# Three edits to the order of work in a two-layer graph and mixture-of-experts kernel: the last pair's shares, the last full block of layer 0, the stores of finished tiles

## The chip, the cores and the metric

The kernel runs on one core of one Trainium2 chip. The metric is the device time of one execution in microseconds (us). Before the change the median of three runs is 1194.18 us, and they lie between 1194.14 and 1195.82. The engines are named as the profile names them: PE (TensorE, matrix products; PEld is its loading of weights), DVE (VectorE), ACT (ScalarE), POOL (GpSimd) and SP (SyncE, which here only starts transfers). A "q" behind a name (SPq, ACTq) is the engine's sequencer, which starts DMA transfers.

## The reference: what is computed

There are N = 3327 nodes with 256 features, padded to 26 tiles of 128. Two layers are computed, each a graph aggregation and then a mixture of eight experts of which each node uses two. In short:

```python
# layer 0
x = x + relu(adj @ (layernorm(x) @ W) + b)
xn = layernorm(x);  top2, idx = top_k(xn @ Wg.T + bg, 2);  p = softmax(top2)
x = x + sum_k p[k] * (relu(xn @ W1[idx_k].T + b1[idx_k]) @ W2[idx_k].T + b2[idx_k])   # hidden 1024
# layer 1
f = tanh(adj * adj) * (adj > 0), only the 700 largest entries of each row kept
x = x + relu(f @ (tanh(layernorm(x) @ Wp + bp) @ Wg1) + bg1)
xn = layernorm(x);  w = softmax(xn @ R.T);  best two, renormalised
x = x + xn + sum_k w[k] * (gelu(xn @ w1[idx_k] + b1[idx_k]) @ w2[idx_k] + b2[idx_k])   # hidden 256
```

All of it is float32.

## The kernel before

**Aggregation.** The adjacency matrix streams through six buffers `ring0` to `ring5` in pieces of 13 x 256 columns. Layer 0 (`aggregate_first`, L482) works on 13 panels of 256 nodes, the inner ones in pairs by Strassen-Winograd with seven half products. The last panel, number 12, is alone: `rest` (L558) goes through its 26 steps of `add` and, at step `first + behind_`, calls `finish`, which weighs the sums of the pair before it (panels 10 and 11) by the weight matrix (`weigh`, L503: products `ps_o`, then `add_relu` on DVE), lists the pair before that one (`listed`), and routes panels 10 and 11 (`route0`: layer norm, scores, ranks). `behind_` is `LAST_BEHIND`, 8 before. Layer 1 (`aggregate`, L430) has the plain form.

**Routing.** A pair of panels is routed on DVE (scores L662, ranks L691 to L717, the difference of the two best scores L727) and listed afterwards by `list_tokens` (L759): ACT takes the exponential of that difference (L762), DVE makes the two shares of it (`shares`, L733 to L738), PE counts the places of each node (`pr`, L770 and L771), DVE turns these into row numbers, and POOL scatters the rows into a list per expert in DRAM.

**Experts.** Blocks of 256 nodes of one expert (128 for the small "single" ones) are run by `step` (L1341) of `experts`, in the order of a plan that is made on the chip. A block is: transposes of its rows (`ptb`, L1172, copied by ACT at L1176), the hidden products `ps_h` (L1224, eight of them in layer 0) each followed by ReLU or GELU on ACT (L1232), and the output products `ps_y`. These have two forms. `second` (L1301) makes two sums of eight products each (L1321) and then adds the bias and weighs by the share on DVE (L1328, L1329). `second_seven` (L1256) takes seven half-size products (L1272); it needs sums of the weights from DVE, made by `prepare` (L1182: t1, t2, t4, t3 at L1191 to L1194, held in the buffer `gate`), sums of the hidden values (`difference` L1215, and L1263 to L1265), and eight additions L1279. Both forms end in `put`: POOL scatters the rows of the output to DRAM (`ys`, L793). Layer 0 has 30 blocks in its usual course, 0 to 29; 12, 17, 22 and 27 are single ones. From block 3 on, all full blocks of layer 0 take the seven products (`seven=3`).

**Around the first block.** Block 0 runs right after panel 12. Its `step` is given `between=finish_last`: the weighing of panel 12, the listing of panels 10 and 11 and the routing of panel 12, traced between the hidden products of block 0 and the transposes of block 1. The transposes `ptb`, `ps_h` and `ps_o` share two PSUM buffers (pool `psh`), so each waits for an earlier one to be read.

**From layer 0 to layer 1.** In the usual arm of a branch (L1723 to L1735) blocks 26 and 27 run, `add_begun` adds the expert outputs of the first 12 tiles to x on DVE (L1410, six additions), block 28 runs, `statistics` makes the layer-norm statistics of these tiles, and block 29 runs. `between` (L1626) then normalises all tiles (L371), transposes them (`pt` L387), and makes the features of layer 1 (`ps_p` L1614, `ps_s` L395). From tile 12 on it first reads the expert outputs back from DRAM (`ring<-ys`, started by SP at L1396), which has to follow all scatters, and adds them (L1410).

**End of layer 1.** In the usual arm (L1752 to L1788) blocks 8 to 31 run. From the count `at` = 18 on (the number of blocks started) SP reads outputs of finished pairs of tiles back, one pair a block; DVE adds the pair two blocks later (`add_loaded`), and ACT starts the store of the finished rows to the output (L1759).

**Order.** The code is traced in program order; then the Tile framework puts each engine's instructions in an order by a schedule of its own, in which something that is ready sooner can be issued before something written earlier. `tc.issue_after(i)`, and `behind(list)` with the last instruction of the list, keep what is traced inside behind instruction i, but only what runs on i's own engine. `last_product` holds PE's last product, `last_hidden` ACT's last ReLU or GELU, `last_y` DVE's last operation on an output. Semaphores follow from the data.

## Time and profile before

| what | us |
|---|---|
| median of three runs (lowest, highest) | 1194.18 (1194.14, 1195.82) |
| the profiled execution, its time | 1194.71 |
| its span, first to last instruction | 1192.9 |
| PE busy in the span | 1152.2 (97%) |
| DVE busy | 871.1 (73%) |
| ACT busy | 557.6 (47%) |
| POOL busy | 295.4 (25%) |

By stages, from the times of the span:

| stage, us | length | PE busy |
|---|---|---|
| 272.0 to 300.0: panel 12 | 28.0 | 27.09 |
| 300.0 to 313.6: block 0 up to its output products | 13.6 | 11.03 |
| 313.6 to 640.0: blocks 0 to 25 | 326.4 | 326.17 |
| 640.0 to 684.5: blocks 26 to 28 | 44.5 | 43.88 |
| 684.5 to 698.8: block 29 | 14.3 | 11.80 |
| 698.8 to 753.0: features of layer 1 | 54.2 | 52.77 |
| 753.0 to 1047.0: aggregation of layer 1 | 294.0 | 294.00 |
| 1047.0 to 1128.0: blocks of layer 1 | 81.0 | 79.94 |
| 1128.0 to 1163.0: blocks of layer 1 beside the read-back | 35.0 | 28.30 |
| 1163.0 to 1193.0: single blocks and the last outputs | 30.0 | 11.41 |

How to read it: a line of the timeline has the start, the duration, the engine, the line of the code, the operation, what it writes and reads, and how often; behind it in brackets the time that the engine stood idle just before, and what ended that. A line of the waits has the total, the number and the longest. One float32 product is two MATMUL records. Idle time of an engine matters only where the work that ends the stage stands behind it.

### The profile page before, as it was taken

Reading aid. Unit: us, or ns where it says so; the run is one execution under the profiler, and the core shown is the slowest. Engines: PE = TensorE matmul, PEld = TensorE weight load, DVE = VectorE, ACT = ScalarE, POOL = GpSimd, SP = SyncE. Lnnn points to the kernel's source line nnn. Section 1 sums busy time; section 2 is a strip of 40 time slices with the busy share of each in tenths; the row PEclk is TensorE's granted clock in tenths of the full one; section 3 lists DMA queues with packets and bytes.
Section 4 is the critical chain, followed back from the end, with each engine's and each line's share of the span. In section 5 each row is a group of like instructions: output and inputs, shape, how many; then the busy total and the mean of one; then the engine's idle time right before and its main releaser. Section 6 shows DMA issues by size and latency. Waiting matters only on the chain. (4 is left out here: it accounts for less than half of the span.)

```text
span 1192.9 us, 19772 instructions
## 1 busy us (share of the span) xinstructions
PE 1152.2 (97%) x6241; PEld 1005.0 (84%) x6241; DVE 871.1 (73%) x3013; ACT 557.6 (47%) x1053; POOL 295.4 (25%) x367
## 2 busy tenths in 40 slices
PE   8999999999999999999999999999999999999973
PEld 7888888888788888888888877888888888888863
DVE  7698999988875555554545669389999998785454
ACT  5689657440223333334333345985564552043321
POOL 2111332243331111111111111022233223265432
PEclk9999999999999999999999999999999999999996
DMA  9995738734376556757575936154454451478686
GB/s 350 178 278 248 250 126 234 252 104 147 122 256 226 187 190 194 259 182 266 191 232 172 370 142 259 63 186 160 167 195 156 180 185 59 130 243 258 209 282 218
DMA packets 123185, 241.68 MB, mean 203 GB/s; under 512 B 24480, under 2 KB 93120, under 8 KB 116160
## 3 DMA queue, kind: packets, MB, share of 16 engines
q1 hardware_dynamic: 108656, 205.59, 52.8%
q0 software_dynamic: 11136, 31.60, 7.1%
q10 hardware_dynamic: 3280, 3.15, 0.8%
q8 instruction: 51, 0.84, 0.3%
q14 instruction: 62, 0.51, 0.1%
HBM read 203.98 MB, written 36.33 MB: 201 GB/s over the span
## 5 line engine op out<-in xcount | busy, mean ns | idle before, releaser
L440 PE MATMUL ps_g<-s,ring 128*128 128x256 f32 x1352 | 294.2, 380 | 0.0
L440 PEld LDWEIGHTS ps_g<-s,ring 128*128 128x128 f32 x1352 | 256.0, 190 | 34.4
L1232 ACT ACTIVATE pad<-ps_h,ring 128x256 f32<-128x256 f32 (+1 forms) x282 | 128.9, 458 | 286.9 <-PE ps_h L1224 147.4
L1224 PE MATMUL ps_h<-pad,ring 128*128 128x256 f32 (+1 forms) x1184 | 254.7, 368 | 4.5 <-ACT pad L1176 4.2
L1224 PEld LDWEIGHTS ps_h<-pad,ring 128*128 128x128 f32 x1184 | 201.1, 191 | 47.3 <-ACT pad L1232 11.5
L793 POOL DMA_INDIRECT ys<-pad,index x114 | 117.0, 1027 | 366.5 <-DVE pad L1279 250.4
L662 DVE SCALAR_TENSOR_TENSOR rt_product<-xn,gate 128x256 f32<-128x256 f32 x400 | 195.4, 488 | 16.1 <-ACT xn L360 2.8
L793 POOL DMA_INDIRECT xlist<-xn,rt_idx x104 | 115.3, 1109 | 153.4 <-DVE ln_nw L347 58.0
L1486 ACT ACTIVATE sign<-ring,below 128x416 bf16<-128x416 f32 x208 | 133.4, 641 | 11.9 <-DMA ring<-in_adjT 6.0
L470 PE MATMUL ps_g<-ring,pad 128*128 128x256 f32 x520 | 115.1, 380 | 2.0 <-DMA ring<-in_adjT 2.0
L470 PEld LDWEIGHTS ps_g<-ring,pad 128*128 128x128 f32 x520 | 98.4, 190 | 15.6 <-DMA ring<-in_adjT 2.4
L1651 ACT ACTIVATE ring<-ring 128x3328 f32<-128x3328 f32 x22 | 65.4, 2977 | 87.4 <-DVE ring L1650 56.3
L1279 DVE SCALAR_TENSOR_TENSOR pad<-ps_y,ring,pad 128x128 f32<-128x128 f32 x184 | 61.9, 348 | 47.9 <-PE ps_y L1272 47.7
L470 PE MATMUL ps_g<-ring,s 128*128 128x256 f32 x390 | 89.6, 379 | 0.0
L470 PEld LDWEIGHTS ps_g<-ring,s 128*128 128x128 f32 x390 | 74.1, 190 | 10.1
L480 DVE TENSOR_TENSOR ring<-ring,ring 128x768 f32<-128x768 f32 (+1 forms) x80 | 79.6, 1013 | 0.0
L495 PE MATMUL ps_g<-ring,s 128*128 128x256 f32 x312 | 68.5, 380 | 3.1 <-ACT s L360 3.1
L495 PEld LDWEIGHTS ps_g<-ring,s 128*128 128x128 f32 x312 | 59.0, 190 | 11.6 <-ACT s L360 3.7
L1652 ACT ACTIVATE ring<-ring 128x3328 f32<-128x3328 f32 x22 | 65.4, 2977 | 0.6
L1263 DVE TENSOR_TENSOR xnT<-pad 128x512 f32<-128x512 f32 x23 | 15.9, 691 | 59.5 <-ACT pad L1232 59.5
L776 POOL COPY xn<-rt_w 128x4 f32<-128x4 f32 x26 | 4.9, 199 | 211.1 <-DVE rt_w L738 211.1
L1321 PE MATMUL ps_y<-s,pad 128*128 128x256 f32 (+1 forms) x200 | 49.6, 388 | 0.1
(240 smaller groups left out, 1595.6 us busy)
## 6 DMA issues: line engine op xcount, KB each, us to landing
ring<-in_adjT SPq DMA_DIRECT2D x50, 1664.0 KB, 8.9
ring<-in_f_w1T SPq DMA_DIRECT2D x30, 1024.0 KB, 5.6
ring<-in_f_w2T SPq DMA_DIRECT2D x30, 1024.0 KB, 9.1
ring<-xlist SPq DMA_DIRECT2D x52, 258.0 KB, 3.5
ring<-in_f_w SPq DMA_DIRECT2D x36, 256.0 KB, 3.6
ring<-ys SPq DMA_DIRECT2D x12, 512.0 KB, 4.7
ring<-in_f_b SPq DMA_DIRECT2D x34, 128.0 KB, 8.2
xlist<-h2T SPq DMA_DIRECT2D x16, 257.0 KB, 13.8
```

The lines of the kernel that those rows point to most:

```text
L440: nc.tensor.matmul(ps[it], lhsT=chunks[k][:, c, ts(it, P)], rhs=s[:, j, :], start=(j == 0), stop=(j == NT - 1),)
L470: nc.tensor.matmul(ps, lhsT=b[:, c, :], rhs=a[:, c, :], start=(first and c == 0), stop=(c == CJ - 1), skip_group_check=not first,)
L480: nc.vector.tensor_tensor(out[:, part, :], out[:, part, :], other[:, part, :], ALU.add)
L495: nc.tensor.matmul(sums[pan][c], lhsT=s[:, j, ts(c, P)], rhs=piece(pan, j // CJ)[:, j % CJ, :], start=(j == 0), stop=(j == NT - 1),)
L662: nc.vector.scalar_tensor_tensor(product, xn, 1.0, gate[:, e, :], ALU.mult, ALU.mult, accum_out=sc[:, g, e : e + 1],)
L793: d = nc.gpsimd.indirect_dma_start(out=a[:, :], out_offset=bass.IndirectOffsetOnAxis(ap=index, axis=0), in_=rows_, in_offset=None,)
L1224: last_product[:] = [nc.tensor.matmul(ps, lhsT=w1[:, c, ts(hc, P)], rhs=xT[:, c, :], start=(c == 0), stop=(c == DC - 1),)]
L1232: nc.scalar.activation(hT[:, hc, :], ps, func, bias=bb1[:, hc : hc + 1])
L1279: last_y[:] = [nc.vector.scalar_tensor_tensor(part, ps, xb[:, g, WT : WT + 1], part, ALU.mult, ALU.add)]
L1486: nc.scalar.activation(sign, piece(pan, k)[:, :, ts(i, GROUP)], AF.Sign, bias=below, accum_out=positive[:, pan, i, k : k + 1],)
L1651: nc.scalar.activation(a, a, AF.Square)
L1652: nc.scalar.activation(a, a, AF.Tanh)
```

## The change

It has three parts.

1. `LAST_BEHIND` goes from 8 to 11: the call of `finish` in panel 12 comes three steps later. And what is traced in `between` of block 0 is no longer kept behind PE's last hidden product, but behind ACT's last ReLU of the block, so the edge now holds for ACT's instructions and no longer for PE's.
2. The range of blocks by seven products ends before the last full block: block 29 of layer 0 takes `second`, with eight products a sum, instead of `second_seven`. The weight sums of block 28 (`prepare`) are traced ahead of `add_begun` instead of inside `step`.
3. The store of a finished pair of tiles in layer 1 is traced two blocks after its addition, not one.

```diff
-BEHIND, LAST_BEHIND = 5, 8
+BEHIND, LAST_BEHIND = 5, 11
...
         def prepare(t):
 
+            if not seven or t not in seven or groups_of(t) < SG:
+                return None
             w2 = loaded[t][4]
...
+        ahead = {}
+
+        def prepare_next():
+
+            t = len(started)
+            ahead[t] = prepare(t)
+
         def step(late, end=always, place=None, between=None):
...
-            sums = prepare(t) if seven and t >= seven and groups_of(t) == SG else None
+            sums = ahead.pop(t) if t in ahead else prepare(t)
             hT = first(ready.pop(t), w1, bb1, groups_of(t), sums)
             if sums:
                 y = weighed_bias(t)
             if between:
-                with behind(last_product):
+                with behind(last_hidden):
                     between()
...
-        nc.scalar.copy, BLOCKS0, seven=3,
+        nc.scalar.copy, BLOCKS0, seven=range(3, EARLY + LATE_PAIRS + FIXED[0] - 1),
...
         layer0.step(late)
         layer0.step(late)
+        layer0.prepare_next()
         with behind(last_y):
             add_begun()
         layer0.step(late)
...
+            def store_added(until):
+                while added and added[0][1] <= until:
+                    t, n = added.pop(0)[0]
+                    nc.scalar.dma_start(out=rows_of(out, t, n), in_=x[:, t : t + n, :])
+
             while len(layer1.started) < layer1.always:
                 layer1.step(late1)
                 at = len(layer1.started)
-                for tiles in added:
-                    nc.scalar.dma_start(out=rows_of(out, *tiles), in_=x[:, tiles[0] : sum(tiles), :])
-                added.clear()
+                store_added(at - 2)
...
                         add_loaded(yt, *tiles)
-                        added.append(tiles)
+                        added.append((tiles, at))
...
-            assert not (waiting or added)
+            assert not waiting
+            store_added(at)
```

More of the change, by code (lines that the diff above doesn't have):

```diff
@@ L1391, in experts @@
             state=state, back_to=back_to, know=know, know_rest=know_rest,
-            turn_first=turn_first, tiers_done=tiers_done(), always=always,
+            turn_first=turn_first, prepare_next=prepare_next, tiers_done=tiers_done(), always=always,
         )
```

## The prediction

> **What bounds the kernel now.** I read the page first: PE is busy for 97% of the span, so what counts is where PE stands, and what follows the last product. Then PE's waits over the whole span, of which these two lie in the stages that the edits touch.

> ```profile
> PE ps_o L506 <- ACT pad L1232: 2.6, 1, 2.6
> PE ps_y L1272 <- DVE gate L1193: 2.5, 1, 2.5
> ```

> The timeline at the first:

> ```profile
> 306.34 0.47 ACT L1232 ACTIVATE pad<-ps_h,ring 128x256 f32<-128x256 f32 x1 [0.39 <-PE ps_h L1224]
> 309.98 0.20 ACT L762 ACTIVATE rt_d<-rt_d 128x4 f32<-128x4 f32 x1 [3.17 <-DVE rt_d L727]
> 310.09 0.46 ACT L1232 ACTIVATE pad<-ps_h,ring 128x256 f32<-128x256 f32 x1
> ...
> 310.60 2.07 PE L506 MATMUL ps_o<-proj_sb,xnT 128*128 128x256 f32 x4 [2.57 <-ACT pad L1232]
> 312.47 0.21 PE L770 MATMUL pr<-rt_both,before 128*128 128x8 bf16 x1
> ```

> ACT stands 3.17 us before the exponential, which waits for DVE; the last ReLU of block 0, whose products ended at 307.17, is behind it, and PE waits for its PSUM buffer. The stage table by microseconds shows what else that costs: PE's clock is halved.

> ```profile
> 311.00:312.00 1.00, 1.00 (x3) 0.77 (x3) 0.63 (x2) 0.00 (x0) 0.25 (x2) 0.50 0.00 0
> ```

> (The 0.50 is the granted clock.) The second wait, in PE's timeline of block 29:

> ```profile
> 689.78 1.05 PE L1272 MATMUL ps_y<-ring,pad 128*128 128x128 f32 x8
> 693.33 1.16 PE L1272 MATMUL ps_y<-gate,pad 128*128 128x128 f32 x8 [2.50 <-DVE gate L1193]
> ```

> and the chain that ended last, after it:

> ```profile
> 707.17 5.63 DMA ring<-ys
> 712.90 1.24 DVE x L1410
> ```

> DVE makes the statistics of 12 tiles (12 x 0.39 us) before block 29's weight sums, and PE stands. The read-back starts only at 707.17, after the last scatter of block 29 (POOL, 701.35), and from 712.90 DVE's chain sets the pace: it asks for tile 12's transpose at 720.22, PE was free at 719.45. Last, the tail:

> ```profile
> 1136.57 0.69 DVE L1410 TENSOR_TENSOR x<-x,ring 128x512 f32<-128x512 f32 x1
> ...
> 1137.30 0.39 ACTq L1759 DMA_DIRECT2D out_x<-x  x1
> ...
> 1137.78 0.59 ACT L1176 COPY pad<-ptb 128x512 f32<-128x512 f32 x1 [2.63 <-DVE pad L1328]
> ...
> 1138.42 1.99 PE L1224 MATMUL ps_h<-pad,ring 128*128 128x256 f32 x8 [1.66 <-ACT pad L1176]
> ```

> The store waits for the addition, the copy stands behind the store, PE behind the copy.

> [...] 2.57 us idle, then half clock from about 310.2 to 313.7. [...] Here the last scatter took 5.82 us from its start to the read-back's (701.35 to 707.17); I use that.

> **Part 1, block 0.** `LAST_BEHIND`: PE's products `ps_o` waited 0.92 us (at 283.15) for DVE's L403; three steps later (12 records x 0.22 = 2.6 us) DVE has caught up, so 0.92 us goes. But panels 10 and 11 reach DVE later. PE came to `finish` at 280.06 and now at 282.7; the last of four L403, at 285.52, needs the fourth `ps_o`, which ends about 282.7 + 0.2 + 16 x 0.25 = 286.9, so near 287.2 with its own wait for L404, and fewer statistics are interleaved. I take +1.45 us for the rest of that DVE chain (bounds 1.0 and 2.6), which has no slack: scores and ranks run from 290.69 to 309.95 almost without a gap. The edge: ACT's last ReLU no longer stands behind the exponential. Block 0's products end at 307.17 - 0.92 = 306.25, the second pair of `ps_o` ends near 307.9. Then PE wants the listing products `pr`, which need DVE's counts: 310.0 + 1.45 = 311.45, in place of 312.47. Gain 1.0 us, if what lies between `pr` and the output products (1.15 us at half clock) stays as it is; the half clock may well come again, for PE idles some 3 us. The wait is so replaced by one for DVE. With the edge gone on PE, though, the framework may let block 0's output products pass `pr`. Then nearly all of the stage's loss could go: without a stall they would start at 307.9 + 0.24 + 0.44 = 308.6 against 313.62. Bounds: a loss of 0.6 us (the transposes of block 1 wait for L403, which stands behind the shares, at 312.6) and a gain of 4. I take 1.0. PE has no other wait until 640, so this shift arrives whole; queued behind ACT's exponential is then only the copy L1176. The moved `finish` also issues eight scatters on POOL (from 283.56, 1.28 us apart); they start some 0.7 us later, and what POOL makes next is not needed before the scatters at 315.48.

> **Part 2, block 29.** Removed from DVE: four weight sums and `difference` (5 x 0.68), three hidden sums (3 x 0.69), eight L1279 (8 x 0.35), in all 8.3 us; added two L1328 and L1329, 2 x (0.42 + 0.35) = 1.5 us. From ACT two L1209 (0.9 us). On PE 56 records at 0.111 (eight every 0.89 us: 694.33, 695.22) are 6.23 us; eight products are 32 at 0.216 (320.55 to 327.46 for 32 records) = 6.91, so 0.68 us dearer. The 2.50 us wait goes. So does 0.56 us at 677.35, where PE waited for ACT's copy because block 28's t4 came only at 678.5: `prepare` of 28 now goes ahead of the six additions (6 x 1.22), done near 673, while the hidden sums, behind the same DVE work as before, come at the same time (covered by block 29's hidden products as fillers; without them about 1 us). From 689.78 to 698.79 PE took 9.01 us; now 6.91. So PE is free for the transposes at 698.79 - 2.10 - 0.56 = 696.1. DVE's statistics end near 692, before that.

> What the end of the stage hangs on is the last scatter: it was held to 701.35 by the last L1279 and by the `gate` load that POOL issued between both scatters (700.46), since block 29 was reading `gate`. Now `gate` is free after block 28, and the scatter follows the last product by 0.20 + 0.46 + 0.63 us (as at 334.81 to 336.10): 697.4. That is 3.9 us earlier; read-back at 703.3, landed 708.9, tile 12 ready at 716.3; PE, 20.66 us of work after 696.1, at 716.8. Then PE's pace of 7.8 us for four tiles meets DVE's 8.05 (720.22, 728.27, 736.32), and after three groups DVE's chain, 3.9 us earlier, decides. The filters of layer 1 are queued behind these same instructions and move along, and the aggregation is all PE (294.00 of 294.00). Gain 3.9 us; bounds 2.0 (if DVE puts block 29's outputs ahead of the normalised tiles, PE waits 1.9 us) and 4.3.

> **Part 3, the stores.** Seven stores of 256 KB, 0.38 us of ACT's queue each, in the same number. All seven stand in the trace where their addition ends; five are issued even before the copy L1176 that is traced ahead of them. So the framework issues a store when it is ready, and tracing it later need not move it. Likeliest value 0. If it does move: ACT no longer stands, PE gains its waits of 3.6 us for L1176 and the 3.1 us before 1163.17. But DVE stays on its loop of scatter, 5.2 us, read-back, 4.2 to 5.9 us, addition. I estimate 2.8 us; bounds -0.5 and 3.5. The last store is traced four blocks before the end, so none delays the final outputs.

> **Sum.** 1.0 + 3.9 + 0 = 4.9 us: the profiled execution from 1194.71 to 1189.8 (span 1188.0), the median, 0.53 us lower, to 1189.3.

> **Rivals.**
> (a) As above: 1189.3, within 1188.0 to 1190.8. Chance 0.40.
> (b) The stores do move: 2.8 us more, 1186.5. For: PE's waits for ACT; against: the order seen in the trace. 0.17.
> (c) Block 0 gives nothing, as `pr` and the half clock take it all (-0.6 to 0.5): 1190.3. For: DVE's gapless chain. 0.15.
> (d) The transition gives half, with DVE's order as the new wait: 1191.7, on the border. Against: normalising is ready 3 us before PE. 0.11.
> (e) The order barely changes, or the gain is lost to transfers: 1193.5. 0.06.
> (f) Slower: without the edge on PE, the `pr` products are issued ahead of block 0's hidden products. PE would stand until 311.5, then do 6.91 + 1.8 + 0.4 us: outputs at 320.6 against 313.62, 7.0 us lost, up to 8.7 with the half clock; 1198. It decides (over 6.3 us lost) if fewer than three of eight hidden units stand ahead of them. For: ACT's order shows that the schedule took DVE's ranks to be ready too early; against: by one unit, not five. 0.11.

> **How the numbers follow.** 0.2%, 2.4 us, is about what a measurement tells from no change: 1191.8 and 1196.6. Faster: 0.40 + 0.17 + 0.15 - 0.02 + 0.04 of (d) = 0.74; same: the rest of (c) and (d), and (e) = 0.15; slower 0.11. The range leaves out (f), the top of (e) and the lowest part of (b): 1185.3 to 1193.4.

> **What would show it.** Part 1: the exponential after the ReLU in ACT's order, no wait at 283, `ps_o` without a wait, and one before `pr`. Part 2: 32 records L1321 in block 29 with no wait; POOL's `gate` load ahead of its scatters; read-back some 4 us earlier against the start of block 29; no PE wait for L371. Part 3: stores still just after their addition. Wrong: `pr` inside the hidden products, DVE's L371 behind L1328, or a shift at 753 that the tail gives back.

## The result, and the profile after

The changed kernel takes 1190.43 us (median of 6 runs, 1188.28 to 1192.74); the kernel before, run beside it, takes 1195.32 us (6 runs, 1194.14 to 1196.85). The ratio is 0.9959, with a 95% interval of 0.9944 to 0.9973: 4.9 us faster. The prediction was 1189.3 us within 1185.3 to 1193.4. The profiled execution of the changed kernel is the slowest of its six: 1192.74 us, with a span of 1191.0 against 1192.9 before, so the pair of profiles shows only 1.9 us. I come back to where the other 3 us are.

PE's waits over the whole span of the changed kernel, the longest in total first (total, number of times, longest):

```profile
PE ps_g L495 <- ACT s L360: 4.4, 2, 2.4
PE ptb L1172 <- ACT pad L1234: 4.2, 3, 3.1
PE ps_h L1226 <- ACT pad L1176: 4.1, 3, 2.6
PE pr L770 <- DVE rt_both L700: 3.1, 1, 3.1
...
PE ps_y L1274 <- DVE xnT L1265: 0.8, 1, 0.8
```

Both waits that the prediction quoted are gone: `ps_o` for ACT's ReLU (2.6) and `ps_y` for `gate` (2.5). Two new ones stand there: `pr` for DVE (3.1), in block 0, and `ps_y` for a hidden sum (0.8), in block 28. (Lines behind the edits are numbered 2 to 10 higher than before: L1232 is now L1234, L1272 L1274, L1321 L1323, L1396 L1405, L1759 L1769.)

Block 0, from PE's and ACT's timelines of the changed kernel (start, duration, engine and line; in brackets the idle time before and what ended it):

```profile
306.71 1.89 PE L506 MATMUL ps_o<-proj_sb,xnT 128*128 128x256 f32 x8
306.91 0.47 ACT L1234 ACTIVATE pad<-ps_h,ring 128x256 f32<-128x256 f32 x1 [0.39 <-PE ps_h L1226]
...
311.67 0.17 PE L770 MATMUL pr<-rt_both,before 128*128 128x8 bf16 x1 [3.07 <-DVE rt_both L700]
...
311.75 1.09 PE L1172 MATMUL ptb<-ident,ring 128*128 128x128 f32 x4
312.64 2.60 PE L1323 MATMUL ps_y<-ring,pad 128*128 128x256 f32 x6
...
313.37 0.21 ACT L762 ACTIVATE rt_d<-rt_d 128x4 f32<-128x4 f32 x1
```

The last ReLU now stands ahead of the exponential L762, and all eight `ps_o` records run without a wait. PE then stands 3.07 us for DVE's counts. The table by microseconds shows the clock after it (the 0.50 is the granted clock, the bracketed counts are instructions):

```profile
312.00:313.00 1.00, 1.00 (x5) 0.98 (x5) 1.00 (x6) 0.12 (x1) 0.14 (x1) 0.50 0.00 0
```

The output products' first six records take 2.60 us, where six at full clock took 1.46 in a second profile of this kernel.

Blocks 28 and 29, and what follows, from the timelines of PE, POOL, SP and DVE of the changed kernel:

```profile
680.86 2.09 PE L1274 MATMUL ps_y<-gate,xnT 128*128 128x128 f32 x16 [0.82 <-DVE xnT L1265]
...
686.81 0.58 POOL L320 DMA_DIRECT2D gate<-gate  x1
...
690.24 7.07 PE L1323 MATMUL ps_y<-ring,pad 128*128 128x256 f32 x32
...
697.15 1.04 PE L387 MATMUL pt<-ident,xn 128*128 128x128 f32 x8
...
698.74 0.97 POOL L793 DMA_INDIRECT ys<-pad,index  x1 [1.67 <-DVE pad L1331]
...
701.42 0.93 SPq L1405 DMA_DIRECT2D ring<-ys  x2
...
707.02 2.49 DVE L1419 TENSOR_TENSOR x<-x,ring 128x1024 f32<-128x1024 f32 x2 [3.66 <-DMA ring<-ys]
```

Block 29 is 32 records in a row; the `gate` load goes out 13.65 us earlier (686.81 for 700.46), the read-back 5.75 us earlier (701.42 for 707.17). From 697.15 to the aggregation at 748.68 PE never waits for DVE again.

The tail, from the timeline of the changed kernel:

```profile
1134.65 0.38 ACTq L1769 DMA_DIRECT2D out_x<-x  x1
1135.13 0.59 ACT L1176 COPY pad<-ptb 128x512 f32<-128x512 f32 x1 [3.55 <-DVE pad L1330]
...
1135.77 1.99 PE L1226 MATMUL ps_h<-pad,ring 128*128 128x256 f32 x8 [2.57 <-ACT pad L1176]
```

It is the picture of before: store, copy, PE behind both. ACT's whole order after 1043 us is, row for row, that of before; and with the line of part 3 set back by one block, every engine's instruction order is compiled the same. Part 3 changed nothing on the chip.

### The profile page after: what moved, and what is told of

Read it like the earlier page. It is cut to its first block, busy times and chain, and to the rows that moved or that the text cites. A ratio compares the mean times of both kernels' runs of the same rounds, so it can differ in the third digit from the quotient of the medians.

```text
span 1191.0 us, 19704 instructions
## 1 busy us (share of the span) xinstructions
PE 1152.0 (97%) x6217; PEld 1005.4 (84%) x6217; DVE 867.1 (73%) x3001; ACT 557.0 (47%) x1051; POOL 290.5 (24%) x367
## 5 line engine op out<-in xcount | busy, mean ns | idle before, releaser
L1234 ACT ACTIVATE pad<-ps_h,ring 128x256 f32<-128x256 f32 (+1 forms) x282 | 128.9, 458 | 287.2 <-PE ps_h L1226 156.1
L1281 DVE SCALAR_TENSOR_TENSOR pad<-ps_y,ring,pad 128x128 f32<-128x128 f32 x176 | 59.3, 348 | 47.5 <-PE ps_y L1274 47.3
L495 PE MATMUL ps_g<-ring,s 128*128 128x256 f32 x312 | 70.2, 386 | 4.4 <-ACT s L360 4.4
L495 PEld LDWEIGHTS ps_g<-ring,s 128*128 128x128 f32 x312 | 60.1, 194 | 13.5 <-ACT s L360 5.2
L1323 PE MATMUL ps_y<-ring,pad 128*128 128x256 f32 x224 | 53.8, 386 | 0.0
```

The costliest lines, as they stand in the source:

```text
L495: nc.tensor.matmul(sums[pan][c], lhsT=s[:, j, ts(c, P)], rhs=piece(pan, j // CJ)[:, j % CJ, :], start=(j == 0), stop=(j == NT - 1),)
L1234: nc.scalar.activation(hT[:, hc, :], ps, func, bias=bb1[:, hc : hc + 1])
L1281: last_y[:] = [nc.vector.scalar_tensor_tensor(part, ps, xb[:, g, WT : WT + 1], part, ALU.mult, ALU.add)]
```

## The experiments

I read each profile by distances that don't contain the program's start, which differs by up to 3 us from run to run (the last panel's first product comes at 270.26 to 273.18, the last chip of these experiments aside). A is from the first product of the last panel (L495) to block 1's hidden products, B from there to block 26's, C from block 26's to the aggregation, E from layer 1's first hidden products to the end; aggregation to layer 1 is 295.25 us in every profile. "Part 2 alone" and "sums ahead alone" were cut from the changed kernel and keep the line of part 3, which moves nothing.

| kernel | A | B | C | E |
|---|---|---|---|---|
| before | 48.26 | 326.43 | 104.77 | 145.9 |
| changed | 47.80 | 326.16 | 101.54 | 147.1 |
| part 1 alone | 47.93 | 326.15 | 106.06 | 146.9 |
| its place behind the ReLU alone | 47.77 | 326.43 | 105.47 | 147.1 |
| part 2 alone | 48.38 | 326.43 | 101.14 | 144.2 |
| eight products alone | 47.68 | 326.43 | 101.25 | 144.6 |
| sums ahead alone | 48.36 | 326.43 | 108.08 | 148.4 |

### Part 1 alone

```diff
-BEHIND, LAST_BEHIND = 5, 8
+BEHIND, LAST_BEHIND = 5, 11
-                with behind(last_product):
+                with behind(last_hidden):
                     between()
```

> Part 1 alone (both of its edits) on the kernel before. Theory A, as in the prediction: 1.0 us faster (0.4 to 1.3): 0.92 us of waiting at 283 gone, and PE stands about 3 us for DVE's counts at 308.6 to 311, so that the output products of block 0 start about 1 us earlier than before. Theory B, read off the trace of the changed kernel, where PE came to block 1's hidden products 0.43 us later than before: it gives nothing, -0.3 to 0.3 us, because DVE's chain of scores moves back by as much as PE gained. What tells them apart in the trace is the distance from the first early wait to the start of block 1's hidden products, with the start of the program, which differs from run to run, taken off: A 1.0 us shorter, B as before.

Measured: 1193.04 us against 1193.62, ratio 0.9991 (0.9976 to 1.0005). By time alone it is not told from nothing. The trace lies between the theories: A varies with where the half clock falls, of which before, the changed kernel and "sums ahead alone" have 3.41 us each (A is 47.68 to 48.38 with the old block 0); it is 48.17 in the mean of those four profiles and 47.88 in the mean of three with part 1, 0.3 us shorter, and B is 0.28 shorter without any such spread: about 0.6 us in all. (A fourth profile with part 1, on another chip, had no half clock there and an A of 46.35; it comes at the end of the experiments.) The 0.28 lies in block 2's hidden products (30 records in 7.09 us before, in 6.81 after), with no wait recorded; its cause stays open. With the edge put back, and the eleven steps kept, every engine's order is compiled the same: beside `LAST_BEHIND = 11` the edit of the edge does nothing.

### The place behind the ReLU, with eight steps

```diff
-                with behind(last_product):
+                with behind(last_hidden):
                     between()
```

> Half of part 1: the shares of the last panel traced behind the last ReLU, the eight steps left as they are. Theory A (the half that matters is the ReLU's place on ACT): PE keeps its 0.92 us wait at 283 but no longer stands 2.57 us for the ReLU; it then stands for DVE's addition that frees the second PSUM buffer, block 1's transposes start at 311.8 against 312.73, so 0.9 us faster, the same as both halves together. Theory B (the half that matters is the wait at 283): within 0.3 us of before, since DVE's chain ends when it did and PE waits for it instead.

Measured: 1193.01 us, ratio 0.9991 (0.9972 to 1.001); A 47.77. PE's waits for DVE in this kernel (the same columns as above):

```profile
PE ptb L1172 <- DVE gnn_t L403: 1.0, 1, 1.0
PE ps_o L506 <- DVE gnn_t L403: 0.7, 1, 0.7
PE pr L770 <- DVE rt_both L700: 0.4, 1, 0.4
```

The wait at 283 stays (0.7), the ReLU's is gone, and PE stands for the addition L403 instead: the two waits of Theory A, and a third of 0.4 us for `pr` that it did not have. The gain on the mean of A is 0.4 us where it said 0.9, and the time alone does not tell it from nothing. By the traces either half of part 1 brings about the same, for either way PE ends up waiting for DVE's chain.

### Part 2 alone

```diff
-    nc.scalar.copy, BLOCKS0, seven=3,
+    nc.scalar.copy, BLOCKS0, seven=range(3, EARLY + LATE_PAIRS + FIXED[0] - 1),
...
+        layer0.prepare_next()
         with behind(last_y):
             add_begun()
```

> Part 2 (and the stores' part 3, which leaves the built order of every engine as it was) on the kernel before. Theory A, as in the prediction: 3.9 us faster (bounds 2.0 to 4.3). Theory B: 3.2 us, the shift that the traces show between 668 us and layer 1's first hidden products; Theory C: all of the 4.9 us, the block-0 part being worth nothing. Read-back of the last outputs 3.9 us earlier by A, over 5 us earlier by B and C; in B what the read-back gains beyond PE's 3 us is lost since PE's work after block 29 is the bound.

Measured: 1189.15 us, ratio 0.9964 (0.9948 to 0.998), so 4.3 us (2.4 to 6.2). C is 101.14. All three theories lie in the interval of the time; the trace decides for more than 3.2 us, because of what the next section shows about the kernel before.

### What the stall of block 29 really costs

The profile of before shows the 2.50 us stall and full clock behind it. Three more profiles of kernels with that stall don't. Here are two stretches of 3.41 us around the stall in before; each line has the length, the busy times of PE, PEld, DVE, ACT and POOL, and then the granted clock:

```profile
689.13:692.54 3.41, 1.70 (x12) 1.43 (x10) 3.41 (x14) 1.74 (x4) 0.00 (x0) 1.00 0.00 1
692.54:695.95 3.41, 2.62 (x23) 2.62 (x24) 3.41 (x15) 0.00 (x0) 0.00 (x0) 1.00 0.00 0
```

The same in part 1 alone:

```profile
690.01:693.42 3.41, 0.90 (x8) 0.72 (x7) 3.41 (x13) 0.66 (x2) 0.00 (x0) 1.00 0.00 0
693.43:696.84 3.41, 3.41 (x18) 3.41 (x18) 2.60 (x12) 0.00 (x0) 0.00 (x0) 0.50 0.00 0
```

The same stall (2.51 us in part 1 alone) is followed by 3.41 us at half clock, and the first transposes come 1.6 us later than in the profile of before, counted from block 26 (53.45 us for 51.81). "Its place behind the ReLU alone" has 53.45 as well; "sums ahead alone", with 2.94 us of stall and 6.83 us at half clock, has 55.40. C with the stall is 104.77, 105.47, 106.06 and 108.08; without it 100.8 to 101.5 in nine profiles. The profile that I predicted from is the cheapest of the four.

The stretches are not chosen at will. In the profile of before, and in that of the changed kernel, all changes of the granted clock lie whole multiples of 3.41 us apart, and before's lines above are cut on that grid; those of part 1 alone are cut where its half clock begins and ends, 3.41 us apart too. What differs between the four cases is how long PE stands within one such stretch. Before's stall is split into 1.71 and 0.79 us; in the other three kernels the stretch ahead of the half clock holds 2.51, 2.50 and 2.28 us of it. In the two profiles of before and of the changed kernel, each of the seven stretches at full clock in which PE stood 2.00 us or more (2.00 to 3.28) is followed by half clock, and none in which it stood 1.94 us or less is. The other profiles don't all keep to these two numbers: at block 0 of "its place behind the ReLU alone" PE's waits are only 0.39 and 1.00 us, and the 32 records of the output products behind them take 8.72 us, for 7.07 at full clock. In the changed kernel's profile 2.92 us of the 3.07 us wait for `pr` lie in one stretch, with half clock behind it (0.50 at 312); in a second profile, on another chip, the wait is 3.13 us and full clock is behind it (1.00 from 311 to 316).

### The two halves of part 2

Eight products alone (`seven=range(...)` as above, without `prepare_next`):

> Part 2's first half alone on the kernel before: block 29 by eight products, block 28's weight sums where they were. Theory A, as in the prediction: the 2.50 us stall is gone and 0.56 us at 677 stays, so 3.3 us faster than before (3.9 less 0.56). Theory B: the sums put ahead win 0.56 us and lose as much to the new wait of 0.4 to 0.8 us for the hidden sum that the traces of the changed kernel and of part 2 alone show; then this kernel reaches PE's first transpose of the normalised tiles as soon as part 2 did, within 0.2 us counted from block 26, and is as fast.

Sums ahead alone:

```diff
+        layer0.prepare_next()
         with behind(last_y):
             add_begun()
```

> Part 2's second half alone: block 28's weight sums put ahead of the additions, block 29 still by seven products. Theory A: 0.56 us faster than before at most, the 2.50 us stall before block 29's second product stays, and with it the half clock behind it (1.5 us more in two of three profiles that have the stall). Theory B: nothing, -0.3 to 0.2 us, since a wait for the hidden sum takes the 0.56 us.

Measured: 1189.28 us, ratio 0.9957 (0.9941 to 0.9973) for the eight products; 1193.97 us, ratio 1.0007 (0.9993 to 1.0021) for the sums. Theory B both times, by the traces (the time of the sums alone would still allow Theory A's 0.56 us). The eight-product kernel reaches its first transposes 49.71 us after block 26, where part 2 alone takes 49.61, though PE still waits at block 28:

```profile
676.27 1.56 PE L1224 MATMUL ps_h<-pad,ring 128*128 128x256 f32 x6 [0.56 <-ACT pad L1176]
```

Its C, 101.25, is as short as with both halves. With the sums ahead this wait goes and that for the hidden sum comes (0.82 above, 0.73 in the sums' kernel). All of part 2's gain is the eight products'.

### The stores really a block later

```diff
-                store_added(at - 2)
+                with behind(layer1.last_hidden):
+                    store_added(at - 2)
```

> The changed kernel, with the stores of part 3 bound on ACT behind the last GELU of the block after which they are traced, so that each of the seven really stands one block later in ACT's order; nothing else differs. Theory A (rival b of the prediction, ACT's wait is what holds PE): 2.8 us faster than the changed kernel (up to 3.5), some 7.7 us faster than before; PE's waits for ACT's copy, 10 us in all after 1128, mostly gone. Theory B (DVE's loop of scatter, landing and read-back is the bound): PE runs ahead, and the last read-backs and the end stay where they are: 0 to 0.5 us faster than the changed kernel.

Measured: 1185.70 us, ratio 0.9931 (0.9908 to 0.9954) to before, against 0.9959 (0.9944 to 0.9973) for the changed kernel: some 3 us more by the medians, though the two intervals touch. Part of this kernel's timeline in the tail:

```profile
1133.71 0.69 DVE L1419 TENSOR_TENSOR x<-x,ring 128x512 f32<-128x512 f32 x1 [2.31 <-DMA ring<-ys]
...
1133.96 0.38 ACTq L1769 DMA_DIRECT2D out_x<-x  x1
...
1134.44 0.58 ACT L1176 COPY pad<-ptb 128x512 f32<-128x512 f32 x1
...
1135.81 1.89 PE L1226 MATMUL ps_h<-pad,ring 128*128 128x256 f32 x8
```

The store at 1133.96 no longer waits for the addition of 1133.71, since it is the one of the block before, and PE's products follow the copy without a wait. E is 142.1 us, and 142.1 in the other kernel with moved stores on these chips (below); in the eight profiles there with the stores unmoved it is 142.9 to 148.4, 145.9 in the mean. One profile's tail thus decides little, but the time, the mean of E and the pair of kernels below, measured on one chip and 3.4 us apart, agree: Theory A, with its 2.8 us. What is left of PE's waits after 1120 is 3.0 us for one GELU and 1.7 us that the profile puts to nothing.

### Block 0 without either wait for DVE

The first attempt puts the last panel's shares in PSUM banks of the output products and lists panels 10 and 11 behind block 0's output products:

```diff
-            ps = psh.tile([P, D], F32, name="ps_o", tag="ph")
+            ps = (psh if pan < NPAN - 1 else psy).tile([P, D], F32, name="ps_o", tag=...)
-            if todo[0][0] == NPAN - 1:
-                listed()
...
     layer0.step(None, between=finish_last)
+    with tc.issue_after(last_product[0].ins):
+        list_tokens(*routed.pop(0))
```

> The changed kernel, with the last panel's shares in PSUM banks of the output products and the listing of panels 10 and 11 traced behind block 0's output products, so that PE meets neither DVE's counts nor the addition that frees a PSUM buffer before them. Theory A (what was left of block 0's stall was DVE's chain, standing on PE through these two waits): output products of block 0 start at 309 in place of 312.6, at full clock, 6.9 us in place of 8.3: 4.5 us faster than the changed kernel (3.5 to 5). Theory B: the wait comes back within the next two blocks, as DVE's chain is late for block 1's outputs or for the list: under 1.5 us.

> The changed kernel with both of the above: stores really a block later on ACT, and block 0's listing behind its output products. If both are apart from each other: 3 us and 4.5 us, so 7.5 us faster than the changed kernel, some 12 us faster than before (1182 to 1183 us). If the tail is bound by a transfer that starts no earlier: 3 us less of it.

Measured: 1193.20 us, ratio 0.9993 (0.9978 to 1.0007), and with the stores moved too 1189.81, ratio 0.9967 (0.9955 to 0.998). Both are slower than expected, by 7 to 9 us. Lines of POOL's, SP's and PE's timelines of the first:

```profile
308.84 7.07 PE L1323 MATMUL ps_y<-ring,pad 128*128 128x256 f32 x32
...
329.88 0.97 POOL L793 DMA_INDIRECT xlist<-xn,rt_idx  x1 [6.44 <-DVE rt_w L738]
...
341.79 0.38 SPq L1136 DMA_DIRECT2D ring<-xlist  x1
...
344.76 1.08 PE L1172 MATMUL ptb<-ident,ring 128*128 128x128 f32 x4 [6.48 <-DMA ring<-xlist]
```

The first half of Theory A came true: output products at 308.84, full clock, A 42.81, 5.0 us shorter. But DVE made the rows' indices only after the last panel's scores (at 328.92), the first scatter to the lists left at 329.88 (317.87 in the changed kernel), and block 3's tokens are loaded behind the last of these scatters. PE stood 6.48 us, at half clock afterwards (the four records of `ptb` take 1.08 us, for 0.60 at full clock); B is 335.67, 9.5 us longer. The pair differs by 3.4 us, once more what the stores bring.

The second attempt binds the list behind the first half of the output products and traces the last panel's routing after the list:

```diff
             if todo[0][0] == NPAN - 1:
-                listed()
+                return
...
+                if halfway and g == 0:
+                    with tc.issue_after(last_product[0].ins):
+                        halfway()
...
-    layer0.step(None, between=finish_last)
+    layer0.step(None, between=finish_last,
+        halfway=lambda: (list_waiting(), list(route0([NPAN - 1]))))
```

> The changed kernel; the last panel's shares in PSUM banks of the output products, and the listing of panels 10 and 11 bound on PE behind the first half of block 0's output products, with the last panel's routing traced after it, so that DVE makes the rows' indices before the last panel's scores and the scatters to the lists go out at about 317, as in the changed kernel, and not at 330. Theory A (the 6.5 us wait of the earlier attempt came from those scatters being late, nothing else): block 1's hidden products start at 316.0 in place of 321.0, block 3's tokens land before PE asks for them at 338, so 5 us faster than the changed kernel. Theory B: the tokens of block 3 are late again, or DVE's L778 stands behind something else; then under 2 us.

> The same, with each store really one block later on ACT. By Theory A and what the stores gave alone (3.0 us): 8 us faster than the changed kernel, 1182 to 1183 us. If the two share a bound in the tail: 5 to 6 us.

> The changed kernel as it is, beside the two above: 4.9 us faster than before (0.9944 to 0.9973 measured already). Its second profile tells what of the first was chance: by my reading the program's start (block 0's stage began 0.8 us late) and the tail (1.2 us longer than before's) vary from run to run, while the distance from the last panel's first product to block 1's hidden products (47.80 us) and from block 26 to the aggregation (101.54 us) are the kernel's own, within 0.2 us.

These three ran on another chip, on which the kernel before takes 1210.50 us; only ratios to it are compared. The changed kernel: 0.9946 (0.9924 to 0.9967), as in the first comparison. The second attempt: 0.9883 (0.9853 to 0.9914). With the stores: 0.9874 (0.9844 to 0.9905), 1195.21 us where the changed kernel takes 1203.40. On this chip both beat the kernel before and the changed one; the gain over the changed one is 6.9 and 8.2 us by medians. PE's timeline of the second attempt:

```profile
308.69 3.62 PE L1323 MATMUL ps_y<-ring,pad 128*128 128x256 f32 x16
...
313.01 0.17 PE L771 MATMUL pr<-cum,ones_sq 128*128 128x8 bf16 x1 [0.65 <-DVE cum L772]
...
313.64 3.70 PE L1323 MATMUL ps_y<-ring,pad 128*128 128x256 f32 x16
317.18 5.13 PE L1226 MATMUL ps_h<-pad,ring 128*128 128x256 f32 x23
```

The scatters to the lists start at 318.99 (329.88 in the first attempt), block 3's tokens are asked for at 331.22, PE doesn't wait for them, and of the 3.1 us for `pr` 0.9 us are left. A is 44.19. That is Theory A's mechanism. In block 2 PE then waits 1.24 us for DVE before the plan's counts (`pc`, L806) and 1.42 us for ACT.

How much of the gain is the order's and how much the chip's is open. From the last panel to block 26 the second attempt takes 373.33 us, the changed kernel 377.25 on this chip, but 373.96 in its first profile. For here the changed kernel stands in block 1, where its first profile has no wait:

```profile
326.14 1.13 PE L1226 MATMUL ps_h<-pad,ring 128*128 128x256 f32 x4 [1.19 <-issue]
328.99 0.66 PE L1172 MATMUL ptb<-ident,ring 128*128 128x128 f32 x4 [1.72 <-issue]
```

("issue" is time that the profile puts to nothing.) So the traces show 3.9 us in this stage on this chip, and 0.6 us against the changed kernel's first profile; the second attempt was not run on the other chips. The stores bring 1.3 us by these medians, but with six runs each, spread over 6 us and more, that is told neither from nothing nor from 3 us. Layer 1 has more idle time on PE here (70 us busy of the 77 from 1043 to 1120, where the other chips show 76); its cause stays open.

My expectation for the second profile of the changed kernel failed in two numbers: A is 46.35 us there and not 47.80, because the clock stayed full (1.00 from 308 to 316), and C is 101.05 for 101.54, which is more than the 0.2 us that I allowed.

## Why the prediction was right

**Part 1: mechanism right, gain too high.** The wait at 283 went, the ReLU went ahead of the exponential, the wait for `pr` came. I had put the ReLU's place down to the edge; the compiled order shows that the eleven steps alone bring it. Block 0's stage began 0.89 us later in the after profile (273.18 for 272.29); without that `pr` is issued at 310.78, against 311.45 predicted, and DVE's scores start 1.38 us later, against 1.45. Output products start 1.87 us earlier. The step that failed is "if what lies between `pr` and the output products stays as it is": the half clock moved from there into the output products, 8.34 us for 6.93, and 1.4 us of it was given back. About 0.6 us remain in the traces of 1.0. The text named the half clock as likely to come again but did not charge for it. That the framework lets output products pass `pr` happened for part of them, but only behind the wait for `pr`, and won nothing.

**Part 2: sum right, two terms wrong.** Between the two profiles C is 3.2 us shorter, not 3.9. The sums put ahead were to save 0.56 us at no cost, "covered by block 29's hidden products as fillers; without them about 1 us": the cover did not hold, the fillers ran earlier, and 0.82 us were lost. The read-back came 5.75 us earlier instead of 3.9, for I priced scatter to read-back at the 5.82 us of before; it took 2.68. The DMA traffic suggests why. Before, 702 to 705 was filled at 344 to 369 GB/s (the last column), the `gate` load (1024 KB) that POOL had issued ahead of the scatter:

```profile
702.00:703.00 1.00, 1.00 (x7) 0.82 (x6) 0.00 (x0) 0.47 (x1) 0.39 (x1) 1.00 0.87 369
...
705.00:706.00 1.00, 1.00 (x6) 0.83 (x5) 0.01 (x1) 0.48 (x2) 0.00 (x0) 1.00 0.28 107
```

Now that load has landed long before. From block 29's last output product to the read-back it is 7.48 to 8.26 us in the four profiles of kernels with seven products there (the additions L1279 lie in it as well), and 4.10 to 4.13 in the nine with eight. The load's place was not moved by itself; that it holds up the scatter's landing is my reading. The extra 1.9 us were worth nothing, since PE and not DVE's chain, as I had written, sets the pace after 697: in its 51.5 us to the aggregation it waits 0.6 us, for ACT. And what the profile of before did not show, the half clock behind the stall in the three other profiles that have it, adds to what the median gains: 4.3 us for part 2 alone, and 4.3 by the mean of C over the profiles with and without the stall ("sums ahead alone", whose stall is longer, left out; 5.0 with it). So 3.9 came out near the truth as the sum of a cost overlooked and a gain overlooked.

**Part 3: right.** The stores did not move. Rival (b), had they moved, said 2.8 us; moved by an edge they brought about 3.

**The sum.** 4.9 us were predicted for 1.0 + 3.9 + 0, and 4.9 measured (3.2 to 6.7 by the interval); the traces have about 0.6, 3.2 to 4.3 and 0. The mechanisms were right, but that the total agrees this closely is luck: part 1 brought less than its term, and part 2, by its own run, more. The profiled pair shows 1.9 us because before's profile had no half clock at block 29, the after profile's block 0 began 0.9 us late, and its tail was the longer one (E 147.1 for 145.9). The rivals: block 0's 0.6 us lie just above the range of (c), -0.6 to 0.5, and below (a)'s 1.0; (d), the handover worth half, and (f), `pr` inside the hidden products, did not come.

## What to carry to other kernels

Price a stall on TensorE with the half clock that may follow it, and look at more than one execution: here the same 2.5 us wait cost nothing more in one profile and 1.6 us more in two others, with 1.71 and 0.79 us of it in two stretches of 3.41 us in the first and 2.51 and 2.50 us in one stretch in the others. An instruction traced later is not yet issued later: look at the order on the engine, and where a store has to follow something, bind it to an instruction of its own engine. Work moved off the path must be followed to its last consumer: the list that was taken out of PE's way came back some 30 us later as a wait for a load.
